# A depthwise convolution's first images loaded side by side, and three of seven tiles of its last normalisation scaled on VectorE

## The chip, the cores and the metric

One core of one Trainium2 chip. The metric is the device time of one execution in microseconds (us). TensorE (PE) multiplies matrices into PSUM, VectorE (DVE) and ScalarE (ACT) work element by element, GpSimd (POOL) does so too and issues indirect DMAs, SyncE (SP) issues most DMAs. Each engine takes its instructions in the order in which the program lists them.

## The reference

The input `x` has 32 images of 128 channels and 56 x 56 points, in float32. Two layers follow each other. The first one is the one that matters here:

```
x = conv_general_dilated(input, dw_kernel, (1, 1), ((3, 3), (3, 3)), feature_group_count=C) + dw_bias
x = transpose(x, (0, 2, 3, 1))
x = (x - mean(x, -1)) / sqrt(var(x, -1) + 1e-06) * ln_gamma + ln_beta
logits = x.reshape(T, C) @ Wg + bg
topv, topi = top_k(logits, 2)
...
return input + x_skip + layer_scale * moe_out
```

So a 7 x 7 depthwise convolution is followed by a normalisation over the channels of each point, and by eight router logits for each point. The two best experts are chosen, points are sorted by their weight and given places in the experts up to a capacity, and the experts (128 to 512 to 128) run on the places. The second layer has a dense and a depthwise convolution and a selective scan over the 3136 points of each image.

## The kernel before, in words

The kernel has four stages, one after another: (1) depthwise convolution, normalisation, logits and the two best experts of each point; (2) routing, which gives every point its places; (3) the scatter of points to the experts, the experts' products and their return; (4) the second layer, most of it the scan. The change lies in stage 1.

**Batches and tiles.** Stage 1 takes the images in eight batches of four (`NB0 = 4`). A tile is 112 points, two image rows, on 112 partitions; an image has 28 of them (`TPI`). Two large tiles in SBUF, `slots2[0]` and `slots2[1]` (named xc in the profile), hold one batch each: for every channel the 29 tiles of each image, the last one of padding. Batch b uses `slots2[b % 2]`, and the convolution's results overwrite its input there.

**fill(b, i)** (line 141) brings in image i of batch b. One DMA (line 144) loads the image, channels on partitions, into `xt`, of which there is one; TensorE transposes it in 29 pieces (line 149) into two PSUM buffers `p_in`, four pieces each, and ScalarE copies each four to the batch's slot (line 151). `xt` has first served for the 7 x 7 taps (lines 133 to 139), which go through it to `taps_d` in DRAM.

**conv(b, c0)** (line 153) does four channels for all four images. The convolution is a matrix product with a banded (Toeplitz) matrix for each channel, `toep`, for two channels at a time. In batch 0 these are built: two DMAs per pair of channels load `raw` from `taps_d` (line 161, three buffers, shared with `xa`), ScalarE copies it to `toep` (line 168, five buffers), and a DMA from GpSimd's queue writes it to `toep_d` (line 169). Later batches load it from there (line 171). Sixteen products per four channels go to PSUM (line 179), and VectorE adds the bias and writes back to the slot (line 183). There are 32 calls per batch.

**norm(b, i, q)** (line 188) takes a group of seven tiles; a batch has sixteen groups. VectorE computes the statistics of each tile (lines 196 and 198), ScalarE a square root (line 200), VectorE its reciprocal `rs` (201) and `nm`, minus mean times `rs` (203). ScalarE then scales the seven tiles one by one to `xa` (line 206, three buffers), GpSimd multiplies by gamma (209) and adds beta (210), a DMA stores the group (212), TensorE transposes it (220), ScalarE copies that (222, two copies per group), TensorE multiplies by the router weights (224), and VectorE adds the router bias to give the logits (228).

**Order.** The loop at line 255 interleaves: beside conv(b) stand norm(b-1) and fill(b+1), spread over the 32 calls. The four fills of batch 0 stand ahead of the loop. In the last turn (b = 8) there is no convolution, and sixteen groups of norm(7) run alone, followed by top2(7), the two best experts. What is written here is not yet the order on the engines: a scheduler in the framework reorders instructions, each engine then runs its own list in order, and waits on semaphores wherever data or a buffer is not ready. Stage 2 begins when the last top2 is done. In it a chain mostly on VectorE ends with the places at line 467, and SP's queue fills the experts' rows with zeros meanwhile (line 286).

Of the kernel before, what the change touches and what calls it, by code (L numbers as in the profile page):

```python
# [5 lines left out]
F32 = mybir.dt.float32  # L6
I32 = mybir.dt.int32
AF = mybir.ActivationFunctionType
ALU = mybir.AluOpType
# [4 lines left out]
C = 128  # L14
RW = C + 2
HW = 56
L = HW * HW
TT = 112
# [21 lines left out]
NB0 = 4  # L40
# [4 lines left out]
def tile_kernel(tc: tile.TileContext, a: dict, out: bass.AP):  # L45
    nc = tc.nc
# [10 lines left out]
    x_d = a["x"].rearrange("n c h w -> n c (h w)")  # L57
    out_d = out.rearrange("n c h w -> n c (h w)")

    with (  # L60
# [15 lines left out]
        for k in (HW - 1, 3 * HW - 1):  # L76
            nc.gpsimd.affine_select(
                out=perm, in_=perm, compare_op=ALU.not_equal, fill=1.0, base=-k, pattern=[[1, TT]],
# [24 lines left out]
        NP = HW // 2  # L103
        with (
# [22 lines left out]

            taps_d = dram.tile([C, TR * TS], F32, name="taps_d")
            toep_d = dram.tile([TT, C, 8, HW], F32, name="toep_d")
            slots2 = [wp.tile([TT, C, NB0 * (NP + 1)], F32, name=f"xc{i}") for i in range(2)]  # L130

            xt = wp.tile([C, (HW + 2) * HW], F32, name="xt")
            nc.gpsimd.memset(xt, 0.0)
            taps = xt[:, : TR * TS].rearrange("c (y x) -> c y x", x=TS)
            dwk = a["L0_conv_dw_kernel"].rearrange("c o h w -> (c o) h w")
# [2 lines left out]
            nc.sync.dma_start(out=taps_d, in_=xt[:, : TR * TS])  # L138
            nc.gpsimd.memset(xt[:, :HW], 0.0)

            def fill(b, i):

                n = b * NB0 + i
                nc.sync.dma_start(out=xt[:, HW : HW + L], in_=x_d[n])
                for j0 in range(0, NP + 1, 4):
                    w = min(4, NP + 1 - j0)
                    p = pin.tile([TT, 4, C], F32, name="p_in")
                    for j in range(w):
                        nc.tensor.transpose(p[:, j, :], xt[:, (j0 + j) * TT : (j0 + j + 1) * TT], ident)
                    o = i * (NP + 1) + j0  # L150
                    nc.scalar.copy(slots2[b % 2][:, :, o : o + w], p[:, :w, :].rearrange("p j c -> p c j"))
# [36 lines left out]
            def norm(b, i, q):  # L188

                w = NP // 4  # L190
                o = i * (NP + 1) + q * w
                xv = slots2[b % 2][:, :, o : o + w]
                st = cp.tile([TT, w, 6], F32, name="st")
                mv = cp.tile([TT, w, 2], F32, name="mv")
                for j in range(w):
                    nc.vector.bn_stats(st[:, j, :], xv[:, :, j])
                for j in range(w):
                    nc.vector.bn_aggr(mv[:, j, :], st[:, j, :])
                rs = cp.tile([TT, w], F32, name="rs")
                nc.scalar.activation(rs, mv[:, :, 1], AF.Sqrt, bias=eps6[:TT])  # L200
                nc.vector.reciprocal(rs, rs)
                nm = cp.tile([TT, w], F32, name="nm")
                nc.vector.scalar_tensor_tensor(nm, mv[:, :, 0], -1.0, rs, ALU.mult, ALU.mult)
                xa = cp.tile([TT, 2 * 8 * TS], F32, name="xa", bufs=3)[:, : w * C].rearrange("p (j c) -> p j c", c=C)
                for j in range(w):
                    nc.scalar.activation(
                        xa[:, j, :], xv[:, :, j], AF.Identity, bias=nm[:, j : j + 1], scale=rs[:, j : j + 1]
                    )
                nc.gpsimd.tensor_tensor(xa, xa, lng.unsqueeze(1).to_broadcast([TT, w, C]), ALU.mult)
                nc.gpsimd.tensor_tensor(xa, xa, lnb.unsqueeze(1).to_broadcast([TT, w, C]), ALU.add)  # L210
                col = (b * NB0 + i) * TPI + q * w
                nc.sync.dma_start(
                    out=res_d[col * TT : (col + w) * TT, :].rearrange("(k p) c -> p k c", p=TT), in_=xa
                )
                pl = plg.tile([TT, w, E], F32, name="p_lg")
                for j0 in range(0, w, 4):
                    g = min(4, w - j0)
                    p = pot.tile([C, 4, TT], F32, name="p_xa")
                    for j in range(g):
                        nc.tensor.transpose(p[:, j, :], xa[:, j0 + j, :], ident[:TT, :TT])  # L220
                    xc = cp.tile([C, 4, TT], F32, name="xc_lg")
                    nc.scalar.copy(xc[:, :g, :], p[:, :g, :])
                    for j in range(g):
                        nc.tensor.matmul(pl[:, j0 + j, :], lhsT=xc[:, j, :], rhs=wg, start=True, stop=True)
                if i == 0 and q == 0:
                    lgs[b] = cp.tile([TT, NB0 * TPI, E], F32, name="lg")
                o = i * TPI + q * w
                nc.vector.tensor_tensor(lgs[b][:, o : o + w, :], pl, bg.unsqueeze(1).to_broadcast([TT, w, E]), ALU.add)
# [22 lines left out]
            NB = N // NB0  # L251
            lgs = {}
            for i in range(NB0):
                fill(0, i)
            for b in range(NB + 1):
                work = []
                for i in range(NB0):
                    if b > 0:
                        work += [(norm, b - 1, i, q) for q in range(4)]
                    if b + 1 < NB:  # L260
                        work.append((fill, b + 1, i))
                if b > 0:
                    work.append((top2, b - 1))
                for k in range(C // 4):
                    if b < NB:
                        conv(b, 4 * k)
                    for w in work[k * len(work) // 32 : (k + 1) * len(work) // 32]:
                        w[0](*w[1:])
# [6 lines left out]
        with (  # L275
# [9 lines left out]
            for k in range(0, E * CAP // 128, ZT):  # L285
# [6 lines left out]
                out=before, in_=ones[:, :128], compare_op=ALU.is_gt, fill=0.0, base=0,  # L292
# [7 lines left out]
            for q in range(QB):  # L300
                p = rp.tile([128, 3, TT], F32, name="p_turn", tag="tot", bufs=3)
# [61 lines left out]
            def total(v, first=None):  # L363

                p = rp.tile([128, v.shape[1]], F32, name="p_tot", tag="tot", bufs=3)
                if first is not None:
                    nc.tensor.matmul(p, lhsT=ones[:, :128], rhs=first, start=True, stop=False)
                nc.tensor.matmul(p, lhsT=ones[:, :128], rhs=v, start=first is None, stop=True)
                return p
# [21 lines left out]
            room = rt.tile([128, E], F32, name="room")  # L391
            for h in range(2):
                p = total(cnts[h])
# [34 lines left out]
            def chosen(i):  # L428
                t = tie[:, i, :]
                r = rs.tile([128, PT], F32, name="junk")  # L430
                nc.vector.tensor_tensor(
                    r.rearrange("j (r t) -> j r t", t=RUN), upto[:, i, :].rearrange("j (r t) -> j r t", t=RUN),
                    over[:, i, :].unsqueeze(2).to_broadcast([128, PT // RUN, RUN]), ALU.is_gt,
                )
                nc.vector.tensor_tensor(r, r, t, ALU.mult)
                nc.vector.scalar_tensor_tensor(
                    t, key[:, i, :], cands[i // HE][:, i % HE : i % HE + 1], r, ALU.is_gt, ALU.add
                )
                scan(i)
                return earlier(upto[:, i, PT - 1 : PT])  # L440
# [14 lines left out]
            p = chosen(0)  # L455
            for i in range(E):
                pn = chosen(i + 1) if i + 1 < E else None
                places(i, p)
                p = pn
# [166 lines left out]
        with (  # L626
# [13 lines left out]
            for q in range(QB):  # L640
                for p0 in range(0, TT, XT):
                    for k in range(2):
# [6 lines left out]
                        for j in range(XT):  # L649
                            apart(nc.gpsimd.indirect_dma_start(  # L650
                                out=buf_d[:, :],
                                out_offset=bass.IndirectOffsetOnAxis(ap=slots[k][:, o + j : o + j + 1], axis=0),
                                in_=xg[:, j, :], in_offset=None,
# [8 lines left out]
        with (  # L662
# [8 lines left out]
                out=lsr, in_=a["L0_conv_layer_scale"].rearrange("c a b -> (c a b)").partition_broadcast(128)  # L671
# [47 lines left out]
            for e in range(E):  # L719
# [10 lines left out]
                for i0 in range(0, CAP, GT * 128):  # L730
# [3 lines left out]
                    for j, m, n in wholes(tiles):  # L734
                        r0 = e * CAP + i0 + j * 128
                        nc.sync.dma_start(
                            out=xb[:n, j:m, :],
                            in_=buf_d[r0 : r0 + (m - j) * n, :].rearrange("(k p) c -> p k c", p=n),
# [4 lines left out]
                    xc = eb.tile([C, GT * 128], F32, name="xc")  # L743
# [510 lines left out]
```

## Time and profile before

| | us |
|---|---|
| median of 3 runs | 16215.65 (16211.88 to 16220.98) |
| the profiled execution | 16201.56 |
| its span | 16199.8 |
| first transpose of the first image | 19.13 |
| first convolution product | 70.20 |
| first scaling of the last batch (line 206) | 1393.05 |
| last logits of stage 1 (line 228) | 1524.89 |
| first scatter (line 650) | 1768.64 |

The profile is that of one execution, whose own time is 16201.56 us; 1.76 us of it lie outside the span. Times in a profile count from the start of the span. A group's row gives line, engine and operation, then what is written and read with shapes, the count, and after the bar the busy time in us and the mean of one in ns. A timeline row gives start, length (of all of its instructions, from the first to the last), engine, line, operation, names, shapes and count, and in brackets the idle time before it and what ended that. TensorE's clock is given as a share of full speed.

### The profile page before, as it was taken

The page shows a single profiled execution, that of the slowest core. Times are in us where ns is not written, and L with a number is a line of the kernel's source. Part 1 is how long each engine was busy: PE and PEld are TensorE (multiplying, and loading weights), DVE is VectorE, ACT ScalarE, POOL GpSimd, SP SyncE. Part 2 cuts the span into 40 slices and gives each one's busy share as a digit, 9 for nine tenths or more (in the row PEclk, how much of TensorE's full clock was granted, in tenths as well). Part 3 has the DMA queues.
Part 4 walks back from the last instruction along what each step waited for, and adds up shares of the span by engine and source line. Part 5 has one row for each costly group of instructions (what it writes and reads, how often), then busy time and mean ns, then how long its engine had stood idle before and what let it go on. Part 6 is the DMA issues. An engine that isn't in the chain of part 4 may idle for free. (4 is left out here: it accounts for less than half of the span.)

```text
span 16199.8 us, 246168 instructions
## 1 busy us (share of the span) xinstructions
PE 12759.5 (79%) x91637; PEld 7021.4 (43%) x91637; DVE 11083.8 (68%) x9909; ACT 10643.5 (66%) x20982; POOL 13611.7 (84%) x9017
## 2 busy tenths in 40 slices
PE   7996100006999989999999999899899999999988
PEld 7995100005777734444444444444444444444443
DVE  2656300001111179999999999999999999999999
ACT  4655100003444478888888888888888888888887
POOL 2443477777888889999999999999999999999999
PEclk9996555558999999999999999999999999999999
DMA  8785433334555555555555555555555555555555
GB/s 266 231 240 195 158 105 102 107 96 69 71 71 72 64 154 175 172 175 176 173 176 174 175 176 174 174 175 175 174 173 175 175 173 176 175 174 175 175 173 162
DMA packets 1239122, 2572.09 MB, mean 159 GB/s; under 512 B 139336, under 2 KB 676640, under 8 KB 1230240
## 3 DMA queue, kind: packets, MB, share of 16 engines
q1 hardware_dynamic: 1041440, 2361.89, 47.1%
q0 software_dynamic: 196480, 194.45, 7.0%
q8 instruction: 721, 11.81, 0.3%
q14 instruction: 481, 3.94, 0.1%
HBM read 2180.38 MB, written 375.43 MB: 158 GB/s over the span
## 5 line engine op out<-in xcount | busy, mean ns | idle before, releaser
L1099 POOL TENSOR_TENSOR db<-du,bb 128x896 f32<-128x896 f32 x3584 | 6847.2, 1934 | 17.6
L1105 ACT ACTIVATE da<-dt,aneg 128x449 f32<-128x449 f32 x7168 | 4577.3, 639 | 269.4 <-DVE prod L1120 86.7
L1114 DVE TENSOR_TENSOR_SCAN da<-da,db 128x898 f32<-128x898 f32 x2240 | 4523.0, 2019 | 2.8 <-ACT da L1105 2.5
L1059 PE MATMUL py<-prod,ident 64*64 64x448 f32 x28672 | 3100.6, 545 | 21.7 <-POOL prod L1120 15.5
L1114 DVE TENSOR_TENSOR_SCAN hs<-da,db 128x898 f32<-128x898 f32 x1344 | 2673.1, 2015 | 487.4 <-ACT db L1126 441.9
L1120 POOL TENSOR_TENSOR prod<-hs,cb 128x896 f32<-128x896 f32 x1344 | 2595.1, 1931 | 459.8 <-PE p_cvc L829 343.6
L1120 DVE TENSOR_TENSOR prod<-da,cb 128x896 f32<-128x896 f32 x2240 | 2446.2, 1092 | 217.6 <-issue 3.5
L744 ACT COPY xc<-ept 128x512 f32<-128x512 f32 (+1 forms) x248 | 143.8, 580 | 2738.9 <-PE ept L742 2738.9
L650 POOL DMA_INDIRECT buf_d<-xg,slot x1568 | 1516.3, 967 | 487.3 <-issue 477.1
L702 POOL DMA_INDIRECT res_d<-ys,xb x984 | 1591.7, 1618 | 333.1 <-issue 285.6
L1059 PEld LDWEIGHTS py<-prod,ident 64*64 64x64 f32 x28672 | 1042.4, 133 | 1446.2 <-issue 1176.9
L742 PE MATMUL ept<-ident,xb 128*128 128x128 f32 (+1 forms) x984 | 188.8, 274 | 1849.0 <-DMA xb<-buf_d 1849.0
L914 PE MATMUL p_xm<-te,wk 128*128 128x448 f32 x3584 | 1415.8, 546 | 1.0 <-DVE te L898 0.6
L694 DVE TENSOR_TENSOR ys<-py,b2t 128x512 f32<-128x512 f32 (+2 forms) x256 | 170.9, 670 | 1679.4 <-PE py L688 1662.6
L647 DVE COPY xg<-gate 128x28 f32<-128x28 f32 x56 | 11.7, 213 | 1746.4 <-DMA buf_d<-xg,slot 1746.4
L688 PEld LDWEIGHTS py<-w2t,hh 128*128 128x128 f32 x7872 | 936.5, 191 | 175.2 <-issue 113.1
L688 PE MATMUL py<-w2t,hh 128*128 128x128 f32 x7872 | 985.2, 278 | 0.2
L914 PEld LDWEIGHTS p_xm<-te,wk 128*128 128x128 f32 x3584 | 658.7, 189 | 730.8 <-issue 572.0
L179 PE MATMUL pc<-xc,toep 112*112 112x112 f32 (+1 forms) x8192 | 935.0, 270 | 35.2 <-ACT toep L168 31.1
L742 PEld LDWEIGHTS ept<-ident,xb 128*128 128x128 f32 (+1 forms) x984 | 124.6, 143 | 1852.7 <-issue 1852.6
L179 PEld LDWEIGHTS pc<-xc,toep 112*112 112x112 f32 x8192 | 878.5, 184 | 45.3 <-ACT toep L168 38.8
L936 PE MATMUL p_z<-te,wz 128*128 128x448 f32 x896 | 522.3, 717 | 466.3 <-ACT xm L930 466.3
(235 smaller groups left out, 19412.9 us busy)
## 6 DMA issues: line engine op xcount, KB each, us to landing
bb<-bc_d SPq DMA_DIRECT2D x1792, 448.0 KB
cb<-bc_d SPq DMA_DIRECT2D x1792, 448.0 KB
toep<-toep_d SPq DMA_DIRECT2D x448, 392.0 KB
xg<-res_d SPq DMA_DIRECT2D x56, 1792.0 KB
buf_d<-zero SPq DMA_DIRECT2D x28, 2275.0 KB
xb<-buf_d SPq DMA_DIRECT2D x240, 260.0 KB
xt<-in_x SPq DMA_DIRECT2D x32, 1568.0 KB
res_d<-xa SPq DMA_DIRECT2D x128, 392.0 KB
```

The costliest lines, as they stand in the source:

```text
L179: nc.tensor.matmul(pc[:, c, :, lo:hi], lhsT=tp[c // 2][:, c % 2, 6 - 2 * o : 8 - 2 * o, :], rhs=s4[:, c, :, lo + o - 1 : hi + o - 1], star ...
L650: apart(nc.gpsimd.indirect_dma_start(out=buf_d[:, :], out_offset=bass.IndirectOffsetOnAxis(ap=slots[k][:, o + j : o + j + 1], axis=0), in_ ...
L688: nc.tensor.matmul(py[:n, j, :], lhsT=hh[:, k, j * 128 : j * 128 + n], rhs=w2t[:, k, :], start=k == 0, stop=k == KF - 1,)
L702: apart(nc.gpsimd.indirect_dma_start(out=res_d[:, :], out_offset=bass.IndirectOffsetOnAxis(ap=xb[:n, j, C + 1 : C + 2].bitcast(I32), axis= ...
L742: nc.tensor.transpose(pt[:, j * 128 : j * 128 + n], xb[:n, j, :C], ident[:n, :n])
L914: nc.tensor.matmul(p[:, :CH1], lhsT=s["wk"][:, k, hs], rhs=d["te"][:, k : k + CH1], start=k == 0, stop=k == DC - 1 and not first,)
L936: nc.tensor.matmul(p[:, :CH1], lhsT=s["wz"][:, h * 128 : (h + 1) * 128], rhs=d["te"][:, DC - 1 :], start=True, stop=True,)
L1059: nc.tensor.matmul(ps[r][h * HD : (h + 1) * HD, :CH1], lhsT=lhsT(rs, h), rhs=rhs[rs, h, :], start=start, stop=stop,)
L1099: nc.gpsimd.tensor_tensor(dbv[i][:, :, 1:], st[g]["du"], units[u].pop("bb"), ALU.mult)
L1105: nc.scalar.activation(da[:, h * W1 : (h + 1) * W1], st[g]["dt"][:, h, :], AF.Exp, scale=s["aneg"][:, h, i : i + 1])
L1114: nc.vector.tensor_tensor_scan(hs, da, dbs[i], 0.0, ALU.mult, ALU.add)
L1120: eng.tensor_tensor(w["prod"], w["hs"][:, :, 1:], w.pop("cb"), ALU.mult)
```

## The change

There are two edits. First, the slot tiles get all 128 partitions (`homes`), and the first batch's four images are loaded into four stretches of the second batch's slot, with their border rows set to zero by VectorE; fill(0, i) transposes out of these and issues no load. From batch 1 on, fill uses `xt` as before, which is free for the first image of batch 1 once the taps are through it. Second, in norm of the last batch, tiles 4 to 6 of each group are scaled by VectorE's tensor_scalar, with the same `rs` and `nm` as per-partition scalars; tiles 0 to 3 stay with ScalarE.

```diff
-            slots2 = [wp.tile([TT, C, NB0 * (NP + 1)], F32, name=f"xc{i}") for i in range(2)]
-
-            xt = wp.tile([C, (HW + 2) * HW], F32, name="xt")
+            homes = [wp.tile([128, C, NB0 * (NP + 1)], F32, name=f"xc{i}") for i in range(2)]
+            slots2 = [t[:TT] for t in homes]
+
+            xt = xt_next = wp.tile([C, (HW + 2) * HW], F32, name="xt")
             nc.gpsimd.memset(xt, 0.0)
...
             nc.gpsimd.memset(xt[:, :HW], 0.0)
 
+            room = homes[1].rearrange("p c t -> p (c t)")
+            first_xt = []
+            for i in range(NB0):
+                t = room[:, i * (HW + 2) * HW : (i + 1) * (HW + 2) * HW]
+                nc.vector.memset(t[:, :HW], 0.0)
+                nc.vector.memset(t[:, HW + L :], 0.0)
+                nc.sync.dma_start(out=t[:, HW : HW + L], in_=x_d[i])
+                first_xt.append(t)
+
             def fill(b, i):
 
                 n = b * NB0 + i
-                nc.sync.dma_start(out=xt[:, HW : HW + L], in_=x_d[n])
+                if b == 0:
+                    xt = first_xt[i]
+                else:
+                    xt = xt_next
+                    nc.sync.dma_start(out=xt[:, HW : HW + L], in_=x_d[n])
...
                 for j in range(w):
-                    nc.scalar.activation(
-                        xa[:, j, :], xv[:, :, j], AF.Identity, bias=nm[:, j : j + 1], scale=rs[:, j : j + 1]
-                    )
+                    if b == NB - 1 and j >= 4:
+
+                        nc.vector.tensor_scalar(
+                            xa[:, j, :], xv[:, :, j], rs[:, j : j + 1], nm[:, j : j + 1], ALU.mult, ALU.add
+                        )
+                    else:
+                        nc.scalar.activation(
+                            xa[:, j, :], xv[:, :, j], AF.Identity, bias=nm[:, j : j + 1], scale=rs[:, j : j + 1]
+                        )
```

## The prediction, made before the changed kernel had run

> **What bounds the kernel now.** I read the page first, then a table of busy times by stretch, then the timeline at both ends of the first stage. The page has the stages in its slices: the depthwise convolution with its norms runs to 1525 us, routing to 1758, the scatter and the expert layer to about 5.7 ms, the scan to the end. The change touches lines of the first stage alone, and past 1540 the instruction order of the changed program is that of the old one on all engines. So only the first 1525 us can change; what they save or lose is carried to the end, because the routing chain on VectorE (1525 to 1758) waits for the last logits, GpSimd's scatter waits for that chain, and the zero fill beside it is issued by 1643, over 100 us early.
>
> At the front, by stretch (us, then busy time of PE, PEld, DVE, ACT, POOL with counts, TensorE clock, DMA share, GB/s):
> ```profile
> 50.00:55.00 5.00, 4.94 (x22) 4.05 (x23) 0.00 (x0) 2.73 (x5) 0.00 (x0) 0.50 0.41 113
> 60.00:65.00 5.00, 1.48 (x7) 1.51 (x8) 0.00 (x0) 0.37 (x1) 0.00 (x0) 0.50 0.47 191
> 65.00:70.00 5.00, 4.18 (x24) 2.56 (x22) 0.00 (x0) 4.26 (x7) 0.00 (x0) 0.85 0.00 0
> 100.00:120.00 20.00, 14.27 (x128) 12.87 (x127) 2.50 (x4) 7.51 (x8) 4.20 (x8) 1.00 0.97 350
> 120.00:140.00 20.00, 14.13 (x129) 12.90 (x128) 2.50 (x4) 7.50 (x8) 4.03 (x8) 1.00 0.98 347
> ```
> Two regimes. Up to 70 us four images pass one after another through one buffer: a load waits for the transposes to release it, then they wait for the load, and DMA idles. From 70 to 237 us the convolution of the first batch keeps DMA 0.95 busy at about 345 GB/s: it builds its Toeplitz tiles from raw taps and writes them back. The tile view of xt says the same of the first regime:
> ```profile
>   DMA xt<-in_x: 43.4, 4
> ```
> This is TensorE's wait for the four image loads. From 240 to 1380 TensorE is the bound (20.00 of 20 us from 1300 on).
>
> At the back, the last batch's sixteen groups of seven tiles run with no convolution beside them. One round, which serves two groups, from the timeline:
> ```profile
> 1429.16 2.13 DVE L203 SCALAR_TENSOR_TENSOR nm<-mv,rs 112x7 f32<-112x7 f32 x2
> 1431.30 2.81 ACT L206 ACTIVATE xa<-xc,nm,rs 112x128 f32<-112x128 f32 x5 [4.03 <-POOL xa L210]
> 1434.76 4.43 ACT L206 ACTIVATE xa<-xc,nm,rs 112x128 f32<-112x128 f32 x8
> 1436.02 2.08 POOL L209 TENSOR_TENSOR xa<-xa,lng 112x896 f32<-112x896 f32 x1 [4.84 <-ACT xa L206]
> 1438.18 2.08 POOL L210 TENSOR_TENSOR xa<-xa,lnb 112x896 f32<-112x896 f32 x1
> 1440.31 1.57 PE L220 MATMUL p_xa<-ident,xa 112*128 112x112 f32 x7 [2.96 <-POOL xa L210]
> 1442.00 2.78 PE L224 MATMUL p_lg<-wg,xc_lg 128*112 128x8 f32 x14
> 1444.82 0.22 DVE L228 TENSOR_TENSOR lg<-p_lg,bg 112x56 f32<-112x56 f32 x1 [6.23 <-PE p_lg L224]
> 1445.18 2.12 DVE L203 SCALAR_TENSOR_TENSOR nm<-mv,rs 112x7 f32<-112x7 f32 x2
> ```
> From L203 to L203 it is 16.02 us for two groups, and no engine is busy through it: it is a ring of latencies. VectorE is in order and L228 of two groups stands ahead of the next L203. ScalarE is charged to POOL, but nm ends at 1431.29, so VectorE's L203 is the one waited for.
>
> **What the Trainium skill says.** "SBUF — State Buffer", section "Who interferes with whom": VectorE and GpSimd share a port pair under an exclusive lock; a VectorE instruction with two SBUF inputs, or in a 2-port mode, blocks fully behind a GpSimd one. The trace agrees: L203 takes 0.15 us at 1392.81, where POOL is idle, and the pair of them 2.13 at 1429.16, ending as POOL's L210 (1429.12 to 1431.19) does. "VectorE: DVE Perf Modes", section "What auto-detection actually checks": one source and destination in SBUF with even outer dimensions give the 2-port mode; a stride isn't among the conditions. So the new tensor_scalar should take the lock too. The nearest row agrees on its speed, not on its lock:
> ```profile
> L542 DVE TENSOR_SCALAR dwd<-ident,dw 128x128 f32<-128x128 f32 x9 | 2.0, 292 | 0.0
> ```
> "TensorE: Matmul & The Clock Gate", section "Part 1: The HAM clock gate (the \"warmup\" mystery)": TensorE runs at half rate until it has been busy through a window. The trace has 0.50 from 1400 to 1525, and the seven transposes take 1.57 us there, 0.83 at full clock (1348.75).
>
> **The change, part by part.** *Images side by side.* Removed: the waits of four loads for the buffer. Moved: in the changed order of SP's queue, image 1 stands before the tap loads, and six constants of the second layer move from there to the end of batch 6; image 2 stands after the taps and, by its wait list, waits for image 1 to land (a semaphore they share); then the tap write, images 3 and 4, and only then raw taps. Image 1 is issued at about 3.1 us (five loads at 0.45 each ahead). An image takes 6.7 to 7.3 us from issue to first transpose (56.75 to 63.52, 11.87 to 19.13), so it is there at 10; image 2 at 17; 3 and 4 follow at 4.6 us each (1.6 MB at 345 GB/s), faster than they are used. One fill takes 5.6 (full clock, the first one less a Toeplitz copy of 0.94) to 6.7 us (the third); I take 6.2. From 17 that is three fills and one copy: 36.5 us for the first convolution, against 70.2: **33.7 us earlier**.
>
> Given back: the old order put five Toeplitz copies and 16 raw loads between the fills, and image 5 too. The new order has one copy. Four pairs (2 x 217 KB raw, 392 KB written) and image 5 (1568 KB) now fall in the DMA-bound regime: 4.9 MB at 345 GB/s, 14 us. Image 5's transposes also stand in one block after eight convolutions instead of between them. At the like block of image 6 (140 to 160, share 0.84) DMA idles 3 us, at image 5's old place 1: 2 us more. Sum: 33.7 - 14 - 2 = **17.5 us saved**. As a check: DMA idles some 31 us of the first 70 before; in the new order I count 3 before image 1, 2 while image 2 waits, 7 while three raw buffers wait for ScalarE, and gaps, some 13. Bounds: 8 (if DMA does no better than 300 GB/s) and 23 (fills at 5.6 and full overlap).
>
> *At nothing:* eight memsets of 56 columns (0.06 to 0.19 us each for rows of this kind) run at 1.4 us, before image 1; a second table load on ScalarE (1.28 at 9.73) stands before the first L200, where ScalarE idles 5.45 us; uncovered it would be 1.3.
>
> *Three of seven tiles on VectorE.* 48 activations (0.56 each in a run) leave ScalarE, 48 tensor_scalars come at 0.29 (bounds 0.2 and 0.4). What counts is the ring. In the new order L228 stands two groups behind, and for two groups in three ahead of the next L203, so groups overlap. I walked that order with the durations above; the same walk of the old order gives 137 us from first statistics to last logits where the trace has 135. POOL's pair of operations becomes the pacemaker, since nm and tensor_scalar can't start while it holds the port. Three steps repeat: nm 0.15, four activations with two copies among them 3.2, POOL 4.25: 7.6; the same without copies, 6.7; and one where the activations ran under POOL and only three tensor_scalars are left, 1.1 + 4.3 = 5.4. That is 19.7 for three groups, 6.6 each, against 8.0. The sixteen end at 114.5 instead of 137: **22.5 us saved**. Queued behind a tensor_scalar that waits are the next group's statistics and, for one group in three, L228; the walk contains both. Bounds: without the lock 26; with TensorE at full clock 28; if one wait more per group on a POOL operation of 2.1 us falls in the ring, 8.7 per group and a loss of 11.
>
> Sum: 17.5 + 22.5 = 40. The profiled execution is 16201.56 (span 16199.8), so 16161.6 on its scale; it lies 14 under the median of three, 16215.65, and against that I forecast **16175.5**.
>
> **Rivals.** (A) As above, 16165 to 16188: 0.58. (B) Tail better: the strided tensor_scalar takes no lock, or TensorE, busy 4.35 of 6.6 us instead of 4.35 of 8.0, gets its full clock: 16155 to 16165. For it: no row shows a strided tensor_scalar against POOL. Against: half clock all through the old tail. 0.14. (C) The tail gives nothing, since one more wait on POOL takes the place of the activations removed: 16198. 0.12. (D) The images do not really come side by side, because each waits on the one before, and the lost head start in Toeplitz tiles eats most of it: start 5, tail 22.5: 16188. 0.08. (E) Slower: the port. If nm and each of the three tensor_scalars is held for a POOL operation of another group, a group takes four holds of 2.1 plus its own 4.25, 12.7 us: +75 in the tail, less 17.5, 16273. It decides from 9.1 us per group, some 1.2 held tensor_scalars per group. Against it: POOL has only one group ready at a time and its two operations follow each other by 0.08 us, so one hold passes both or none. 0.08.
>
> **Numbers.** 0.2%, about what a measurement of this kernel can tell from no change, is 32 us: 16183 to 16248. Faster: most of A, B: 0.68. Same: the rest of A, C, most of D: 0.24. Slower: E, 0.08. The range runs from B to C: 16155 to 16200.
>
> **What would show it.** First convolution at 36 to 38 us and the end of the first batch's convolution at 219 instead of 237; DMA share near 0.95 from 40 on. In the tail L209 every 6.6 us on average, tensor_scalars of 0.3 us that stretch to 2 beside POOL, and last logits 40 us earlier than 1525. I am wrong if tensor_scalar ends with POOL's operations several times per group, or if DMA idles after 40 us.

## The result, and the profile after

The changed kernel takes 16178.17 us, median of nine executions (16147.44 to 16203.23); the kernel before, run beside it, 16215.65 (16205.61 to 16236.96). The ratio is 0.9975, 95% interval 0.9964 to 0.9985, so some 37 us, or 0.25%, less. The forecast was 16175.5. The profiled execution took 16167.26 us, with a span of 16165.5.

Executions of one kernel spread by 31 us (before) and 56 us (after), more than each half of the change is worth. I therefore read the parts from landmarks in the trace. In the changed kernel's lines fill's loads are L148 and L158 (L144 before), its transposes L163 (149), the raw loads L175 (161), the products L193 (179), statistics L210 and L212, nm L217 (203), tensor_scalar L222, ScalarE's scaling L226 (206), gamma L229 and beta L230 (209, 210), and the router bias L248 (228).

| landmark, us | before | after | difference |
|---|---|---|---|
| first transpose | 19.13 | 11.58 | -7.55 |
| first convolution product | 70.20 | 36.40 | -33.8 |
| last bias add of the first batch (L197, L183 before) | 236.87 | 221.18 | -15.7 |
| seventh batch's choice of experts done ("less", its start) | 1387.83 | 1383.37 | -4.5 |
| last logits | 1524.89 | 1497.77 | -27.1 |
| the tail: the row above it less the one before | 137.1 | 114.4 | -22.7 |

The rows behind the table, four of before and then three of after (the first product after stands below):
```profile
70.20 2.02 PE L179 MATMUL pc<-xc,toep 112*112 112x112 f32 x17 [0.51 <-ACT xc L151]
236.87 0.62 DVE L183 TENSOR_TENSOR xc<-pc,dwb 112x448 f32<-112x448 f32 x1 [4.65 <-PE pc L179]
1387.83 0.27 DVE L249 TENSOR_TENSOR less<-v 112x112 f32<-112x112 f32 x1
1524.89 0.22 DVE L228 TENSOR_TENSOR lg<-p_lg,bg 112x56 f32<-112x56 f32 x1 [7.19 <-PE p_lg L224]
...
221.18 0.62 DVE L197 TENSOR_TENSOR xc<-pc,dwb 112x448 f32<-112x448 f32 x1 [5.28 <-PE pc L193]
1383.37 0.26 DVE L269 TENSOR_TENSOR less<-v 112x112 f32<-112x112 f32 x1
1497.77 0.22 DVE L248 TENSOR_TENSOR lg<-p_lg,bg 112x56 f32<-112x56 f32 x1 [5.02 <-PE p_lg L244]
```

**The front.** TensorE's timeline:
```profile
18.76 1.06 PE L163 MATMUL p_in<-ident,xc 128*112 128x128 f32 x8 [1.30 <-DMA xc<-in_x]
...
30.05 1.09 PE L163 MATMUL p_in<-ident,xc 128*112 128x128 f32 x8 [0.52 <-ACT xc L165]
36.40 3.79 PE L193 MATMUL pc<-xc,toep 112*112 112x112 f32 x35 [0.25 <-ACT xc L165]
```
After the first image only the second is still waited for, 1.30 us; from there the fills pass without a wait on a load, held only by ScalarE's copies out of PSUM. TensorE's waits for loads of these four images come to 12.9 us, where they were 43.4. The table of busy times by stretch, with the columns of the prediction's (the last two are DMA share and GB/s):
```profile
20.00:30.00 10.00, 7.73 (x50) 5.16 (x50) 0.00 (x0) 8.52 (x16) 0.00 (x0) 1.00 0.96 362
30.00:40.00 10.00, 8.12 (x64) 6.58 (x65) 0.02 (x1) 8.40 (x13) 1.88 (x3) 1.00 0.44 127
40.00:50.00 10.00, 6.54 (x50) 6.36 (x50) 1.23 (x2) 2.81 (x3) 1.57 (x3) 0.78 0.91 288
50.00:60.00 10.00, 8.14 (x69) 7.79 (x68) 1.25 (x2) 2.82 (x4) 1.84 (x4) 0.88 0.94 325
60.00:80.00 20.00, 16.47 (x124) 15.26 (x123) 2.50 (x4) 6.73 (x9) 3.42 (x7) 0.83 0.99 364
75.00:95.00 20.00, 15.09 (x127) 13.28 (x126) 1.88 (x3) 9.28 (x14) 2.69 (x6) 0.97 0.90 312
120.00:140.00 20.00, 14.58 (x114) 12.41 (x112) 1.25 (x2) 9.25 (x13) 2.63 (x5) 0.91 0.79 261
```
The idle DMA of the old front (share 0.41 to 0.47, then none) is gone but for 30 to 40, where no more than three raw buffers can be filled ahead and ScalarE is busy 8.4 of 10 us with the fills. From there to the end of the first batch DMA is loaded as it was before: share 0.93 at 317 GB/s from 36.4 to 221, 0.94 at 324 from 70 to 237 before. Two holes are left where an image's transposes stand in one block: image 5's from 78 to 84 us (in the row 75 to 95) and image 6's from 127 to 134 (in the row 120 to 140).

**The tail.** GpSimd's timeline counts the groups: one L229 and one L230 each, and the bracket on L229 is what GpSimd waited. Of before:
```profile
1426.96 2.08 POOL L209 TENSOR_TENSOR xa<-xa,lng 112x896 f32<-112x896 f32 x1 [2.73 <-ACT xa L206]
1429.12 2.07 POOL L210 TENSOR_TENSOR xa<-xa,lnb 112x896 f32<-112x896 f32 x1
...
1436.02 2.08 POOL L209 TENSOR_TENSOR xa<-xa,lng 112x896 f32<-112x896 f32 x1 [4.84 <-ACT xa L206]
...
1442.98 2.07 POOL L209 TENSOR_TENSOR xa<-xa,lng 112x896 f32<-112x896 f32 x1 [2.72 <-ACT xa L206]
```
Two groups take 16.02 us: 8.5 of work and 4.84 + 2.72 of waiting for ScalarE's seven activations. The same of the changed kernel:
```profile
1403.64 2.08 POOL L229 TENSOR_TENSOR xa<-xa,lng 112x896 f32<-112x896 f32 x1 [3.22 <-DVE st L210]
...
1410.33 2.09 POOL L229 TENSOR_TENSOR xa<-xa,lng 112x896 f32<-112x896 f32 x1 [2.46 <-ACT xa L226]
...
1417.88 2.08 POOL L229 TENSOR_TENSOR xa<-xa,lng 112x896 f32<-112x896 f32 x1 [3.32 <-ACT xa L226]
...
1424.57 2.08 POOL L229 TENSOR_TENSOR xa<-xa,lng 112x896 f32<-112x896 f32 x1 [2.45 <-ACT xa L226]
1426.73 2.08 POOL L230 TENSOR_TENSOR xa<-xa,lnb 112x896 f32<-112x896 f32 x1
1429.96 2.08 POOL L229 TENSOR_TENSOR xa<-xa,lng 112x896 f32<-112x896 f32 x1 [1.15 <-PE p_xa L240]
```
The steps are 6.7, 7.55, 6.7 and 5.4 us, and GpSimd still waits 1.0 to 3.3 before each group. Added up over all sixteen groups, the idle time between GpSimd's operations is 57.0 us before and 35.8 after, so nearly all of the tail's 22.7 us are waits of GpSimd that are gone. VectorE's timeline shows the new instruction away from and beside GpSimd:
```profile
1408.15 1.03 DVE L222 TENSOR_SCALAR xa<-xc,rs,nm 112x128 f32<-112x128 f32 x3
...
1426.93 2.35 DVE L222 TENSOR_SCALAR xa<-xc,rs,nm 112x128 f32<-112x128 f32 x2
```
At 1408.15 GpSimd is idle and three take 1.03: 0.39 to 0.40 each, one behind the other every 0.32. At 1426.93 L230 runs, from 1426.73 to 1428.81, and two take 2.35: the first ends at 1428.96, just after L230, and the second takes 0.40. Five of the 48 are held in this way, about 2 us each. So the strided tensor_scalar is held by GpSimd's operations, as the prediction took it to be. It is not alone: in the tails of all fourteen profiles of this case, every nm or tensor_scalar that starts more than 0.02 us into a GpSimd operation and more than 0.02 before its end ends after it (177 of 177). VectorE's statistics take 0.37 to 0.42 us even in the midst of such an operation (599 of them), and reciprocals and router biases aren't held either.

### The profile page after: what moved, and what is told of

Same layout as the page of the kernel before. It is cut to its first block, busy times and chain, and to the rows that moved or that the text cites. A ratio compares the mean times of both kernels' runs of the same rounds, so it can differ in the third digit from the quotient of the medians.

```text
span 16165.5 us, 246237 instructions
## 1 busy us (share of the span) xinstructions
PE 12760.0 (79%) x91637; PEld 7032.2 (44%) x91637; DVE 11102.3 (69%) x9965; ACT 10625.4 (66%) x20935; POOL 13616.7 (84%) x9017
## 5 line engine op out<-in xcount | busy, mean ns | idle before, releaser
L193 PE MATMUL pc<-xc,toep 112*112 112x112 f32 (+1 forms) x8192 | 946.5, 271 | 42.8 <-ACT toep L182 39.5
L193 PEld LDWEIGHTS pc<-xc,toep 112*112 112x112 f32 x8192 | 889.1, 185 | 53.4 <-ACT toep L182 47.8
```

Source lines behind the costliest of these rows:

```text
L193: nc.tensor.matmul(pc[:, c, :, lo:hi], lhsT=tp[c // 2][:, c % 2, 6 - 2 * o : 8 - 2 * o, :], rhs=s4[:, c, :, lo + o - 1 : hi + o - 1], star ...
```

## The experiments

"Tail" is the stretch of the table's last row. "The walk" is the prediction's way of working out the tail: each kernel's own order on every engine is followed step by step with the durations of the trace before, an instruction starting when its engine, its data, its buffer and the port are free. In the prediction it gave 137 for the kernel before and 114.5 for the changed one.

### Each half alone

The front alone: the diff above without its last part.

> Only the images side by side; all seven tiles of the last batch stay with ScalarE. If the two gains are separate and add up (my theory), this is the front's share: the last bias add of the first batch at 219 to 221 us instead of 237, from the first scaling of the last batch to the last logits 132 us as before, and 15 to 18 us less in total, ratio 0.9990. If the gain of the front is lost again in the middle (between the first and the seventh batch's choice of experts the changed kernel's profile took 994.0 us where the one before took 984.6), the total is only 5 to 8 us less and that stretch is again 994. If that stretch is chance of one execution, it lies anywhere from 984 to 994 here.

Measured: 16198.25 us against 16217.7 beside it, ratio 0.9987 (0.9980 to 0.9994). Last bias add of the first batch 223.65, later than the 219 to 221 expected and at the upper end of what profiles with this front show (217.3 to 223.7, below); tail 137.1; from the first to the seventh choice of experts 986.5.

The tail alone: only the last part of the diff, on the kernel before.

> Only the scaling of three tiles in seven on VectorE in the last batch; the images pass through one buffer as before. My theory: from the first scaling to the last logits 109 us instead of 132, in links of 7.6, 6.7 and 5.4 us, and 22 us less in total, ratio 0.9986. The rival that the tail gives nothing by itself: 132 us and no change in total. The middle stretch as before, 984.6 us, if the layout of the slots is what slowed it; anywhere from 984 to 994 if it is chance.

Measured: 16192.76 us, ratio 0.9987 (0.9980 to 0.9993). Tail 114.2, last bias add of the first batch 239.81, the middle stretch 991.8.

The halves save 19.5 and 25 us, together 44; both at once saved 37, which the intervals allow. By landmarks they are separate: the tail is 137.1 or 114.2 whatever the front is. The middle stretch is not slowed by the new layout of the slots: with the old layout it took 984.6 in one profile and 991.8 in the one of the tail alone (mean 988.2), with the new one 984.4 to 994.0 in twelve profiles of this case (mean 988.7).

### VectorE's instructions without the relief

```diff
                     nc.scalar.activation(
                         xa[:, j, :], xv[:, :, j], AF.Identity, bias=nm[:, j : j + 1], scale=rs[:, j : j + 1]
                     )
+                    if b == NB - 1 and j >= 4:
+                        sx = cp.tile([TT, C], F32, name="spare_x", bufs=3)
+                        nc.vector.tensor_scalar(sx, xv[:, :, j], rs[:, j : j + 1], nm[:, j : j + 1], ALU.mult, ALU.add)
```


> As the changed kernel, but ScalarE scales all seven tiles of each last group, and VectorE's three scalings are done a second time into a tile that nothing reads. So the instructions are added without any relief of ScalarE, and the order on VectorE goes back to groups in pairs. My theory (the relief of ScalarE, and the order that lets groups overlap, carry the gain): the tail takes 137 us by my walk, 132 to 140, so only the front's 15 to 18 us are saved in total, ratio 0.9990. The rival that the gain of the tail came from anything else, such as instructions of VectorE that shift the holds of the port: about 109 us and 38 us less in total. The rival that added tensor_scalars are each held by GpSimd (the slower case of the prediction): tail well over 150 us.

Measured: tail 137.1; 16193.29 us, ratio 0.9986 (0.9980 to 0.9993), an interval that includes the front's 15 to 18 us. The row of the added instructions, from 1395 to 1490:
```profile
L225 DVE TENSOR_SCALAR spare_x<-xc,rs,nm 112x128 f32<-112x128 f32 x36 | 12.2, 406 | 0.0
```
48 extra instructions on VectorE cost nothing, and without relief of ScalarE there is no gain. The slower rival (E) needed each to be held for 2.1 us; the mean is 0.41. One of the 48 is held, 2.19 us, though GpSimd never touches its tile; so the hold does not come from a shared buffer. But relief and order went away together here, so this leaves open which of them counts.

### One, two and five tiles

The changed kernel with another split, here one tile:

```diff
-                    if b == NB - 1 and j >= 4:
+                    if b == NB - 1 and j >= 6:
```


> As the changed kernel, but VectorE scales one tile of seven. In proportion to the tiles taken from ScalarE (22.7 us for three) the tail would be 129.5. The walk of this kernel's order gives 116.8, so most of the relief comes with the first tile: steps of two groups in 13.4 us.

Measured: tail 117.3, and 16159.90 us in one execution. With two tiles (`j >= 5`):

> As the changed kernel, but VectorE scales two tiles of seven in the last batch instead of three. In simple proportion to the activations taken from ScalarE the tail would be longer than the changed kernel's 114.4: 122. My theory is that the order and the ring decide: the walk of this kernel's order gives 108.4, since groups come in overlapping pairs there (steps of 2.8 and 9.0 us). So 107 to 110 if the walk is right, 122 if relief in proportion is.

Measured: tail 106.1 (16154.67 us). With five (`j >= 2`):

> As the changed kernel, but VectorE scales five of the seven tiles in the last batch (2 to 6) instead of three. The tail, from the start of the subtraction that ends the seventh batch's choice of experts to the last logits, took 137.1 us in the kernel before and 114.4 in the changed one; all tails of these runs are counted in that way. My walk of this kernel's own order, with the same durations as in the prediction, gives 113.1. If ScalarE's share of a group were what counts in simple proportion (22.7 us for three tiles in seven), two more tiles would bring 15 us more: 99. If each tensor_scalar cost a wait on GpSimd, the tail would be longer than 114 by some 2 us a group: 145.

Measured: tail 115.2 (16177.36 us).

With none, one, two, three and five tiles the tail is 137.1, 117.3, 106.1, 114.4 and 115.2; the walk had 137, 116.8, 108.4, 114.5 and 113.1. That is not proportional to ScalarE's relief, and not even monotonic: three tiles are worse than two. Each count gets another order from the scheduler, so order matters as well.

### Relief and order apart

In two kernels the order of the last batch on VectorE and ScalarE was set by hand, with dependencies that order instructions on an engine without a wait (the two lists are left out here):

```diff
+            for order in (
...
+            ):
+                prev = None
+                for w in order.split():
...
+                        if prev is not None:
+                            tc.add_manual_dep(
+                                ins, prev.name,
+                                mybir.DependencyInfo(mybir.DependencyClass.NoSync, mybir.DependencyReason.DATA),
+                                reason="order",
+                            )
+                        prev = ins
```
The first has the relief with the old order: VectorE's list is that of the kernel before, with nm of two groups side by side, and each nm is followed at once by its three tensor_scalars (another place for them was not tried). On ScalarE the copies stand after four and after eight scalings of a pair.

> As the changed kernel with its three tensor_scalars per group, but VectorE and ScalarE take the last batch's instructions in the order of the kernel before, where nm of two groups stand side by side and the router bias of both stands ahead of the next two. The prediction held the new order, in which groups overlap, to be what the gain comes from. If so, the tail is longer than the changed kernel's 114.4, 120 or more. My walk of this order says the opposite, 104.0: two groups in 10.6 to 11.6 us, so the relief of ScalarE alone is worth 33 us, and the new order costs 10 of them.

Measured: tail 106.2, and 16160.97 us in one execution. GpSimd's timeline:
```profile
1424.15 2.09 POOL L234 TENSOR_TENSOR xa<-xa,lng 112x896 f32<-112x896 f32 x1 [3.32 <-DVE xa L227]
1426.32 2.09 POOL L235 TENSOR_TENSOR xa<-xa,lnb 112x896 f32<-112x896 f32 x1
1428.37 2.08 POOL L234 TENSOR_TENSOR xa<-xa,lng 112x896 f32<-112x896 f32 x1
1430.53 2.08 POOL L235 TENSOR_TENSOR xa<-xa,lnb 112x896 f32<-112x896 f32 x1
1435.93 2.08 POOL L234 TENSOR_TENSOR xa<-xa,lng 112x896 f32<-112x896 f32 x1 [3.32 <-DVE xa L227]
```
Here L234 and L235 are gamma and beta, L227 is the tensor_scalar. Two groups take 11.8 us. GpSimd works on both without a pause and waits 3.32 once for the pair, where the changed kernel has it wait before every group. The holds are gone as well. The rows of nm from 1385 to 1480, first of the changed kernel and then of this one:
```profile
L217 DVE SCALAR_TENSOR_TENSOR nm<-mv,rs 112x7 f32<-112x7 f32 x15 | 16.8, 1121 | 0.0
L223 DVE SCALAR_TENSOR_TENSOR nm<-mv,rs 112x7 f32<-112x7 f32 x15 | 2.8, 190 | 0.0
```
The changed kernel's order puts 15 of its 16 nm under an operation of GpSimd, the paired order one.

The counterpart has the changed kernel's order, and ScalarE scales all seven tiles.

> The counterpart: the order of the changed kernel on VectorE and ScalarE in the last batch, but all seven tiles scaled by ScalarE and no tensor_scalar. If the order alone carries the gain, the tail is near 114; the walk gives 125.5, so 12 us of gain from the order when ScalarE is loaded; if the order is worth nothing without the relief, 137.

Measured: tail 124.9 (16176.71 us in one execution).

| tail, us | old order | new order |
|---|---|---|
| seven tiles on ScalarE | 137.1 | 124.9 |
| four on ScalarE, three on VectorE | 106.2 | 114.4 |

The relief alone is worth 31 us, the order alone 12, but the two do not add: with the relief the new order costs 8. Once ScalarE has only four tiles, the second group of a pair is ready while GpSimd works on the first, and pairing hides its whole preparation. The idle time of GpSimd follows: 57.0, 44.7, 27.3 and 35.8 us for no change, order alone, relief alone and both. The tail less this idle time is 78 to 80 us in all four, and in the kernels with one, two and five tiles too.

### GpSimd's share

The changed kernel, with beta left out in the last batch:

```diff
-                nc.gpsimd.tensor_tensor(xa, xa, lnb.unsqueeze(1).to_broadcast([TT, w, C]), ALU.add)
+                if b < NB - 1:
+                    nc.gpsimd.tensor_tensor(xa, xa, lnb.unsqueeze(1).to_broadcast([TT, w, C]), ALU.add)
```


> As the changed kernel, but in the last batch GpSimd's addition of beta is left out, so that GpSimd has one operation of 2.1 us for each group instead of two; this is part of the computation that is left out. If GpSimd's pair is the pacemaker of every link, as the prediction put it, each of the sixteen groups saves 2.15 us: tail 80. My walk, which also has the matrix products, the copies and the router bias in the ring, gives 101.4: the ring has another bound right behind, the chain through TensorE and ScalarE's copies to VectorE's bias addition. If GpSimd is hidden, 114.

Measured: tail 101.5 (16151.06 us in one execution). Half of GpSimd's work, 34 us, is gone, and the tail is 12.9 us shorter. So GpSimd's pair is not the pacemaker of every link; behind it the rest of the ring binds almost at once. (The scheduler's order changed with it, too, so the 12.9 is not GpSimd's share alone.)

### What limits the first batch

The changed kernel, with the first 16 Toeplitz pairs written twice:

```diff
+            spare_d = dram.tile([TT, 32, 8, HW], F32, name="spare_d")
...
                         nc.gpsimd.dma_start(out=toep_d[:, c : c + 2], in_=t)
+                        if c < 32:
+                            nc.gpsimd.dma_start(out=spare_d[:, c : c + 2], in_=t)
```


> As the changed kernel, but the first 16 Toeplitz pairs of the first batch are written to DRAM twice, the second time to a place that nothing reads: 16 transfers of 401 KB, 6.4 MB more. If the first batch's convolution is limited by transfers at 345 GB/s (the step of the prediction by which 14 us are given back), its last bias add comes 18.6 us later, at 240 instead of 221 (238 to 243). If TensorE, ScalarE or the buffers set the pace, 0 to 5 us later. Bounds between them mean that the transfers are only part of the limit.

Measured: first product at 36.49, last bias add of the first batch at 234.07 (16183.38 us in one execution). That is 12.9 us after the changed kernel's 221.18, or 13.7 after 220.4, the mean of nine profiles with the changed kernel's front (217.3 to 223.7). So about 0.7 of the 18.6 us that the added bytes take at 345 GB/s are paid for (0.56 to 0.9, if the new front alone may lie anywhere in its spread); the rest can have gone into idle stretches of DMA. From 36.4 to 110, where the second writes fall, DMA has a share of 0.98 at 340 GB/s, where the changed kernel has 0.94 at 322: the transfers fill this stretch, so a longer hold on the toep buffers isn't what costs the time there. Transfers are most of the limit, not all of it.

The other way round, some of the lost head start was to be won back:

```diff
...
             for i in range(NB0):
                 fill(0, i)
+                if i >= 2:
+                    build(4 * i - 8)
+                    build(4 * i - 6)
```
Here build(c) loads, copies and writes one Toeplitz pair, as conv does for the others; ScalarE's copies are kept in program order.

> As the changed kernel, but ScalarE's copies of the first two Toeplitz pairs stand between the fills of the third and the fourth image instead of one in the fourth fill, so that raw buffers come free while the fills run. In the changed kernel the DMA share falls to 0.44 from 30 to 40 us, some 5 us of lost transfer. If what is given back is Toeplitz building in a stretch limited by transfers (my theory), the share from 30 to 40 rises to 0.7 or more, the last bias add of the first batch comes 2 to 4 us earlier than 221, though the first convolution product comes about 1 us later, and the total is 2 to 4 us below the changed kernel, hardly to be told from it. If instead ScalarE or TensorE sets the pace there, the end moves later by the 1 us.

Measured: first product at 37.46, 1.06 later, as expected. Its row of the table by stretch:
```profile
30.00:40.00 10.00, 7.80 (x42) 6.14 (x43) 0.00 (x0) 8.98 (x14) 2.31 (x4) 0.72 0.60 192
```
The DMA share rose from 0.44 to 0.60, less than the 0.7 expected. Last bias add of the first batch at 218.87, total 16173.84 us, ratio 0.9974 (0.9963 to 0.9984). The 2.3 us lie within the 6.3 us by which profiles with one and the same front differ. Whether this helps stays open.

### The parts together

Two Toeplitz pairs between the fills, three tiles on VectorE and the paired order:

> The two best parts together: images side by side with two Toeplitz copies between the third and the fourth image's fills, three tiles on VectorE, and the paired order of the last batch. If the parts add up as the walk and the runs so far say, 2 us of the front and 10 of the tail on top of the changed kernel: some 50 us below the kernel before, 16168, ratio 0.9969. If the paired order is worse than the changed kernel's, at or above the changed kernel's 16178.

Measured: 16161.7 us against 16214.59 beside it, ratio 0.9967 (0.9955 to 0.9979); tail 106.2, last bias add of the first batch 219.32. This is the fastest of the versions that were timed repeatedly. Its interval overlaps that of the changed kernel; the 8 us of the tail between them are read from the traces.

## Why the prediction was right, and where its reasons were not

**The front, 33.7 us earlier: right.** The first product came 33.8 us earlier. That it came out to 0.1 us is luck, since two errors cancelled: image 1 was there at 11.58 and not at 10, image 2 at 18.76 and not at 17, but a fill takes 5.5 to 5.9 us and not 6.2.

**Given back, 14 + 2: right as a sum.** 33.8 less 15.7 is 18.1 in the two profiles; with 220.4 for the new front (nine profiles) and 238.3 for the old one (236.87 and 239.81) the net gain is 17.9, where 17.5 was forecast, so 16 were given back. That the cause is Toeplitz building in a stretch bound by transfers is supported by the doubled write, in which 0.7 of the added time was paid for. The split of the 16 was a little off. The prediction read the first batch's convolution as a share of 0.95 at about 345 GB/s; over 70 to 237 it is 0.94 at 324, and at that rate its 4.9 MB take 15 us and not 14. Image 5's transposes in one block leave DMA idle for 2.0 us from 75 to 95, where the old place (80 to 100 before) left 1.2, so this term is 1 us rather than 2. Both are estimates from one profile each. Winning some of it back was too small to see.

**At nothing: right for the table load.** The second load takes 1.28 us at 218.63, and ScalarE then still waits 4.79 us for the first statistics. The memsets stand within VectorE's 0.95 us of work in the first 10 us, before the first image.

**The tail, 22.5 us: right in size.** The walk counted from the first statistics: 137 before and 114.5 after. Counted in that way the traces have 135.9 (the prediction read 135) and 113.2, which is 22.7 us less where 22.5 was forecast, and the links are the 7.6, 6.7 and 5.4 us that it named. A tensor_scalar takes 0.40 us where it isn't held, which is the upper bound given, and not 0.29. Set beside nine different tails as they are counted here, the walk was off by 2.3 us at most.

**Its reason: half wrong.** The prediction said that in the new order L228 stands two groups behind, "so groups overlap", and that "POOL's pair of operations becomes the pacemaker". Neither holds as put, though the walk, which had relief, holds and order in it together, gave the right sum. The relief alone, in the old order, gives 31 us, and the new order takes 8 of them away. And with half of GpSimd's work gone, only 12.9 of 34 us follow: each link is 4.2 us of GpSimd and a wait of 1.0 to 3.3 for the next group, and that wait is what differs from kernel to kernel. Before, it was 7.6 us per pair; in the changed kernel 3.6 to 5.8 for two groups in a row; in the paired order 3.3. I had walked one order for the relief and not asked what the old one would give.

**The lock: right.** "SBUF — State Buffer", section "Who interferes with whom", and "VectorE: DVE Perf Modes", section "What auto-detection actually checks", were taken to cover a strided tensor_scalar: 0.40 us alone and two in 2.35 beside L230 agree. What the lock costs in total wasn't measured apart. In the paired order the tensor_scalars hardly meet GpSimd, 0.41 us on average against 0.57 in the changed kernel; with two tiles they are held most, 1.08 us (means from 1385 to 1480). Counting nm too, holds add up to some 25 us of VectorE's time in the changed kernel, 1 in the paired order and 26 with two tiles, with tails of 114.4, 106.2 and 106.1. So holds alone don't set the tail: what counts is whether GpSimd waits for them.

**The rivals.** B needed TensorE at full clock in the tail or no lock: the clock is 0.50 from 1390 to 1490 in the changed kernel too. C (the tail gives nothing) fell by the tail alone, D (only 5 us at the start) by the landmarks, E by the copies into a spare tile and by the count: 5 of 48 tensor_scalars are held, where it needed more than one per group.

**The forecast's scale.** The changed kernel's profile shows 27.1 us at the last logits, not 40, as its middle stretch took 994.0 us against 984.6. Fourteen profiles of this stretch, in which no kernel changes anything, lie between 984.4 and 994.0, with the two of the old layout at 984.6 and 991.8; so those 9 us are within the spread of single executions. As a whole the profiled execution is 34.3 us shorter than the one before, because the stages behind the last logits, which the change does not touch, took 7.1 us less in it; in the fourteen profiles they take 14667.5 to 14679.0 us. The medians give 37.

## What to carry to other kernels

Where an engine with fixed work per group lies in a ring, write down what it waits before each group: that wait is what a change on the engines beside it can take away. A change that moves work between engines also moves the scheduler's order, and the two effects need not add: of the two orders compared here, the better one before the relief was the worse one after, so impose the old order once and compare. When an effect is smaller than the spread of executions, differences of landmarks within a stage settle it (the same tail came out within 0.3 us in different executions), while a median of 21 executions against 60 told each half, 0.13%, from nothing, but left its size between some 10 and 32 us.

## What was not expected of the hardware

The stretch of six batches whose instructions are the same in all kernels varied by 9.6 us between executions, 1%, while the tail repeated to 0.3 us: 137.1 in three kernels with ScalarE scaling all tiles in the old order, 114.1 to 114.4 in four with the changed kernel's tail, 106.2 in two with the paired order. In the first stretch TensorE is nearly always busy (1093 of 1140 us from 240 to 1380 in the kernel before) and the granted clock moves; in the tail the clock stood at 0.50 throughout:
```profile
1410.00:1430.00 20.00, 12.62 (x62) 11.65 (x63) 16.59 (x58) 10.05 (x23) 12.52 (x7) 0.50 0.19 51
1450.00:1470.00 20.00, 13.30 (x65) 11.92 (x65) 17.36 (x63) 10.32 (x23) 12.85 (x7) 0.50 0.25 65
```
That the moving clock is the cause of the spread is in part supported: the mean granted clock of the stretch was 0.947 in the longest (994.0 us, the changed kernel) and 0.958 in the kernel before (984.6), and over the fourteen profiles clock and length have a correlation of -0.70. But the shortest, 984.4 us, had 0.953, so the clock does not order them all, and the cause is not shown.
